# A graph layer and attention, in Winograd products: p1 written by ScalarE into the second group's PSUM bank, another order around v, q and k and of the first loads, and a last projection in plain products

**Chip, cores, metric.** One Trainium2 chip, the kernel on 1 core. The metric is device time in microseconds, the median of several executions.

## The reference, cut

```python
# x (32, 512, 512) f32, adj (512, 512) int32 of 0 and 1, about 1 in 32 set; all weights 512 x 512
def reference(x, adj, W, b, Wq, bq, Wk, bk, Wv, bv, Wo, bo):
    # layer 0
    mi, mj = x @ W[:, :512].T, x @ W[:, 512:].T
    a = adj.astype(x.dtype); deg = a.sum(axis=1)
    x = layernorm(x + deg[None, :, None] * (mi + b) + einsum('ij,bjo->bio', a, mj))
    # layer 1: 8 heads of 64
    q, k, v = heads(x @ Wq.T + bq), heads(x @ Wk.T + bk), heads(x @ Wv.T + bv)
    attn = softmax(where(adj == 0, -inf, q @ k^T / 8))
    return layernorm(x + (attn @ v) @ Wo.T + bo)
```

## The kernel before

Everything is written in the order in which each engine runs it; the schedule is by hand. A 512 x 512 product is done as seven products of 256-wide quarters (Winograd's form) in place of eight. `piece` issues one of the seven. Products 1 and 2 form group X, products 6, 7 and 4 group Y, products 5 and 3 group Z; a group adds up in one PSUM bank and each intermediate sum is read out. Product 1, p1, is needed in all three other quarters. Each of the banks a and b exists once.

```python
    def mm_tile(bank):
        return psum.tile([P, 512], FT, name="mm" + bank, bufs=1)
    GROUP = {1: "X", 2: "X", 6: "Y", 7: "Y", 4: "Y", 5: "Z", 3: "Z"}

    def piece(kind, b, i, bank):
        g = GROUP[i]
        first = (kind, b, g) not in OPEN
        if first:
            OPEN[kind, b, g] = mm_tile(bank)
        pm = OPEN[kind, b, g]
        # ... (the operands: a weight piece from the ring, a quarter or a combination)
                    nc.tensor.matmul(pm[:, c * Q:(c + 1) * Q], lhs, rhs, start=first, ...)
                    first = False
        if i == 1:
            p1 = OPEN[kind, b, "p1"] = work([P, 2, Q], "p1", 3)
            nc.scalar.copy(p1, pm)
        # ... l0, pj: GpSimd adds p1 to three quarters, VectorE adds pm to its quarter
        # ... v, q, k: product 2 is read out by ScalarE; in 6, 7, 4 VectorE adds pm and p1

    def phase_c(n):                     # v, q, k of batch n; m = n - 2 is the older batch
        # ...
        res = [norm[0], norm[1], z(apply, n, 1), z(add_bo, n, 0), pc("v", n, 1, "a")]
        if m >= 0:
            res += [z(stats, m, 1)]
        res += [pc("q", n, 1, "b"), pc("v", n, 2, "a"), pc("q", n, 2, "b")]
        if m >= 0:
            res += [z(apply, m, 1)]     # two normalisations on ScalarE; apply(m, 0) is in phase_b
        res += [norm[2], z(combos, ..., (1, 2), 0), pc("k", n, 1, "a"), norm[3], ..., pc("k", n, 2, "a")]
        if m >= 0:
            res += [z(store, m)]
        for i in ORDER[2:]:             # 6, 7, 4, 5, 3
            res += [pc("v", n, i, "a"), pc("q", n, i, "b")]
            # ...
```

`norm` are the transposes of the normalised batch, `apply` normalises two of a batch's four row blocks on ScalarE, `add_bo` adds the output bias on GpSimd, `combos` are the sums of quarters on GpSimd. In `kind`, l0 is layer 0's product (two weights, so each of its seven products takes 16 matmuls in place of 8) and pj the last projection. `told` are sums by which the kernel checks at its end whether its fast path was allowed. `ring` tiles hold weight pieces on their way to TensorE; `e` tiles hold the exponentials of the scores.

Of the kernel before, what the change touches and what calls it, by code (L numbers as in the profile page):

```python
# [25 lines left out]
def gnn_attention_kernel(  # L26
# [98 lines left out]
    nc.sync.dma_start(adj_i, rows(adj))  # L125
    wo = work([P, NC, D], "xh", 3)
    load_x(0)
    W = {}
    W["wj"] = load_w(big(), wjT, nc.scalar)
    W["wi"] = load_w(big(), wiT, nc.scalar)  # L130
    W["wv"] = load_w(work([P, NC, D], "v", 2), wvT, nc.sync)
    W["wq"] = load_w(work([P, NC, D], "v", 2), wqT, nc.scalar)
# [5 lines left out]
    nc.gpsimd.memset(mhalf, -0.5)  # L138
    b0_r = load_row("b0_r", b0)
# [5 lines left out]
    nc.gpsimd.tensor_scalar(bq_c, bq_c, QSCALE, 1.0, op0=OP.mult, op1=OP.mult)  # L145

    adj_f = big()
    nc.vector.tensor_copy(adj_f, adj_i)
# [13 lines left out]
    deg_c = const.tile([P, NC], FT, name="deg_c")  # L162
    nc.vector.reduce_sum(deg_c, adj_f, axis=AX.X)
# [8 lines left out]
    nc.scalar.copy(adjR, adjT)  # L172
# [19 lines left out]

    RING = 12
# [5 lines left out]
    def combine(name, eng):  # L199
        w = W[name]  # L200
        if name == "wq":
            nc.scalar.mul(w, w, QSCALE)
        a11, a12, a21, a22 = [w[:, 2 * j:2 * j + 2, Q * i:Q * i + Q] for i in range(2) for j in range(2)]
        s1, s2, s3, s4, n22 = [ring_tile() for _ in range(5)]
        eng.tensor_tensor(s1, a21, a22, op=OP.add)
        eng.tensor_tensor(s2, s1, a11, op=OP.subtract)
        eng.tensor_tensor(s4, a12, s2, op=OP.subtract)
        eng.tensor_tensor(s3, a11, a21, op=OP.subtract)
        nc.scalar.mul(n22, a22, -1.0)
        for i, t in ((1, a11), (2, a12), (6, s2), (7, s3), (4, n22), (5, s1), (3, s4)):  # L210
            WS[name, i] = dram.tile([P, 2, Q], FT, name=f"{name}_{i}")
            nc.sync.dma_start(WS[name, i], t)

# [112 lines left out]
    def piece(kind, b, i, bank):  # L326
# [4 lines left out]
        pm = OPEN[kind, b, g]  # L331
        terms = []
# [17 lines left out]
        p1 = OPEN[kind, b, "p1"]  # L350
        f, n = {1: (0, 0), 2: (0, 0), 6: (0, 1), 3: (0, 1), 4: (1, 0), 7: (1, 1), 5: (1, 1)}[i]
        if kind in ("l0", "pj"):
            y = XT[b]
            if i == 1:
                for n, f in ((1, 0), (1, 1), (0, 1)):
                    d = quarter(y, n, f)
                    nc.gpsimd.tensor_tensor(d, d, p1, op=OP.add)  # L357
            else:
                d = quarter(y, n, f)
                nc.vector.tensor_tensor(d, d, pm, op=OP.add)  # L360
        elif kind == "v":
            if i == 1:
                V[b] = work([P, NC, D], "v", 2)
            d = quarter(V[b], n, f)
            if i == 2:
                nc.scalar.copy(d, pm)
            elif i in (6, 7, 4):
                nc.vector.tensor_tensor(d, pm, p1, op=OP.add)
            elif i != 1:
                nc.vector.tensor_tensor(d, d, pm, op=OP.add)  # L370
        else:
            T, bias = (QT, bq_c) if kind == "q" else (KT, bk_c)
            if i != 1 and (b, f) not in T:
                T[b, f] = work([P, 2, N], kind, 3)
            if i in (6, 7):
                nc.vector.tensor_tensor(T[b, f][:, :, Q * n:Q * n + Q], pm, p1, op=OP.add)
            elif i != 1:
                for c in range(2):
                    d = T[b, f][:, c, Q * n:Q * n + Q]
                    bc = bias[:, 2 * f + c:2 * f + c + 1]  # L380
                    if i == 2:
                        nc.scalar.activation(d, pm[:, c, :], AF.Identity, bias=bc, scale=1.0)
                    else:
                        o = p1[:, c, :] if i == 4 else d
                        nc.vector.scalar_tensor_tensor(d, pm[:, c, :], bc, o, op0=OP.add, op1=OP.add)
# [4 lines left out]
    def scores(b, hp, kc):  # L390
# [7 lines left out]
        nc.scalar.activation(ps, ps, AF.Exp)  # L398
# [48 lines left out]

    PC, TR, GA = 1.73, 0.44, 1.9
# [11 lines left out]
    def phase_a(n):  # L460
# [4 lines left out]
        for i in range(max(len(g), len(k))):  # L465
            res += k[i:i + 1] + g[i:i + 1]
            if i == 1 and g:
# [20 lines left out]
    def phase_b(n):  # L488

        m = n - 2  # L490
        if n >= B:
            res = []
            for i, bank in ALONE:
                if i == 6:
                    res += [FLUSH, z(combos, TO, m, ot_quarter(m), (1, 2, 3, 4))]
                res.append(pc("pj", m, i, bank))
            return res + [z(stats, m, 0), z(stats, m, 1), z(apply, m, 0), z(apply, m, 1), z(store, m)]
        if m < 0:
            res = []
            for i, bank in ALONE:  # L500
                res.append(pc("l0", n, i, bank))
                if i == 4:
                    res += [z(stats, n, 0)]
            return res + [z(apply, n, 0), z(stats, n, 1)]
        res = []
        for i in ORDER:
# [10 lines left out]
            if i == 3:  # L517
                res.append(z(apply, m, 0))
        return res

    def phase_c(n):
# [4 lines left out]
        res = [norm[0], norm[1], z(apply, n, 1), z(add_bo, n, 0), pc("v", n, 1, "a")]  # L526
        if m >= 0:
            res += [z(stats, m, 1)]
        res += [pc("q", n, 1, "b"), pc("v", n, 2, "a"), pc("q", n, 2, "b")]
        if m >= 0:  # L530
            res += [z(apply, m, 1)]
        res += [norm[2], z(combos, TH, n, h, (1, 2), 0), pc("k", n, 1, "a"), norm[3], z(combos, TH, n, h, (1, 2), 1),
                z(combos, TH, n, h, (3, 4), 0), z(combos, TH, n, h, (3, 4), 1), z(add_bo, n, 1), pc("k", n, 2, "a")]
        if m >= 0:
            res += [z(store, m)]
        for i in ORDER[2:]:
            res += [pc("v", n, i, "a"), pc("q", n, i, "b")]
            if i == 4 and n + 1 < B and n > 0:
# [4 lines left out]

    PERIODS = [phase_a(0) + phase_b(0) + phase_c(0) + phase_a(1)]
    PERIODS += [phase_b(n) + phase_c(n) + phase_a(n + 1) for n in range(1, B)]
    PERIODS += [phase_b(B) if B > 1 else [], phase_b(B + 1)]
    for f in sum(PERIODS, []):
        if f[1] is piece:
            KEYS.extend((name, f[4]) for name in NAMES[f[2]])
# [3 lines left out]

    combine("wj", nc.gpsimd)
    combine("wi", nc.vector)

    edge = const.tile([P, NC, N], BF, name="edge")
    nc.vector.tensor_scalar(edge, adjT, 0.0, None, op0=OP.not_equal)
    nc.vector.tensor_tensor(adj_f, adjT, adjR.bitcast(FT), op=OP.not_equal)
    nc.vector.reduce_sum(told[:, B * HP:], adj_f.rearrange("p c i -> p (c i)"), axis=AX.X)  # L560
    nc.vector.tensor_scalar(told[:, B * HP:], told[:, B * HP:], 2.0 * SAFE, None, op0=OP.mult)
    combine("wv", nc.gpsimd)
    combine("wq", nc.vector)
    combine("wk", nc.gpsimd)

    pd = mm_tile("b")
    bv_w = work([P, DC, P], "big", 6)
    for dc in range(DC):
        nc.vector.tensor_scalar(bv_w[:, dc, :], ones, bv_c[:, dc:dc + 1], None, op0=OP.mult)
        nc.tensor.matmul(pd, bv_w[:, dc, :], W["wo"][:, dc, :], start=(dc == 0), stop=(dc == DC - 1))  # L570
    nc.vector.tensor_add(bo_r, bo_r, pd)
    combine("wo", nc.vector)
# [4 lines left out]
    STEPS = 2 * HP  # L577
    for n in range(1, B + 2):
        b = n - 1
        todo = PERIODS[n]  # L580
        total, done, at = sum(f[0] for f in todo), 0.0, 0
        extra = []
        for step in range(STEPS):
            if b < B:
                hp, half = divmod(step, 2)
                scores(b, hp, 2 * half)
                scores(b, hp, 2 * half + 1)
                if step > 0:
                    ph, phalf = divmod(step - 1, 2)
                    values(b, ph, phalf)  # L590
                    if phalf == 1:
                        sums(b, ph)
                        extra = rest(b, ph)
            if step == 0 and b > 0:
# [3 lines left out]
            late = [(presum, hp, half)] if b < B else []  # L598
            while at < len(todo) and done < total * (step + 1) / STEPS - 1e-6:
                if todo[at] is FLUSH:  # L600
                    while extra:
                        g = extra.pop(0)
                        g[0](*g[1:])
                else:
                    run(todo[at])
                done += todo[at][0]
                at += 1
                if todo[at - 1][0] > 0.0:

                    for g in late + (extra if step == 0 else extra[:1]):  # L610
                        g[0](*g[1:])
                    late, extra = [], [] if step == 0 else extra[1:]
# [3 lines left out]
        for f in todo[at:]:  # L616
            if f is not FLUSH:
                run(f)


    tot = const.tile([P, 1], FT, name="tot")
    nc.vector.reduce_sum(tot, told, axis=AX.X)
    pd = mm_tile("a")
    nc.tensor.matmul(pd[:, 0:1], ones, tot, start=True, stop=True)
    nc.vector.tensor_scalar(tot, pd[:, 0:1], SAFE, None, op0=OP.is_lt)
    again = const.tile([P, 1], I32, name="again")
    nc.vector.tensor_scalar(again, tot, -1.0, 1.0, op0=OP.mult, op1=OP.add)
    fast.close()
    flag = nc.values_load(again[0:1, 0:1], min_val=0, max_val=1)
    with tc.If(flag > 0), tc.tile_pool(name="general", bufs=1) as pools.work:  # L630
# [15 lines left out]
        nc.vector.tensor_scalar(nan_c, nan_c, 0.0, None, op0=OP.mult)  # L646

# [6 lines left out]
        with tc.For_i(0, B, 1) as b:  # L654
# [22 lines left out]
            for hp in range(HP):  # L677
                c = slice(hp * P, (hp + 1) * P)
                qt, kt = work([P, N], "q", 1), work([P, N], "k", 1)
                for t, w, bias, by in ((qt, wq, bq_c, QSCALE), (kt, wk, bk_c, 1.0)):  # L680
# [80 lines left out]
```

## Time and profile before

| | before |
|---|---|
| time | 4076.63 us median of 3 (4075.16 to 4078.4) |
| span of the profiled execution, mean clock | 4072.7 us, 0.992 |
| start to the first scores | 137.0 us |
| first scores to the last batch's first scores (31 batches) | 3823.8 us, 123.35 each |
| from there to the end | 111.9 us |

TensorE is busy for 95% of the span, so a change can win only in the 5% in which it waits. The lines are in the prediction. The three stretches of the table are read from the PE timeline, as the start of a score product (`sc<-q,k`) is easy to find.

### The profile page before, as it was taken

The page shows a single profiled execution, that of the slowest core. Times are in us where ns is not written, and L with a number is a line of the kernel's source. Part 1 is how long each engine was busy: PE and PEld are TensorE (multiplying, and loading weights), DVE is VectorE, ACT ScalarE, POOL GpSimd, SP SyncE. Part 2 cuts the span into 40 slices and gives each one's busy share as a digit, 9 for nine tenths or more (in the row PEclk, how much of TensorE's full clock was granted, in tenths as well). Part 3 has the DMA queues.
Part 4 walks back from the last instruction along what each step waited for, and adds up shares of the span by engine and source line. Part 5 has one row for each costly group of instructions (what it writes and reads, how often), then busy time and mean ns, then how long its engine had stood idle before and what let it go on. Part 6 is the DMA issues. An engine that isn't in the chain of part 4 may idle for free.

```text
span 4072.7 us, 47394 instructions
## 1 busy us (share of the span) xinstructions
PE 3878.7 (95%) x17442; PEld 2655.8 (65%) x17442; DVE 2604.5 (64%) x3514; ACT 1058.0 (26%) x1486; POOL 1889.5 (46%) x2010
## 2 busy tenths in 40 slices
PE   6999999999999999999999999999999999999996
PEld 4766666666666666666666666666666666666663
DVE  3576666666666666666666666666666666666665
ACT  2222222222222222222222222222222222222221
POOL 5444544545445445345454454453454444444533
PEclk8999999999999999999999999999999999999998
DMA  8333333233333333332333333333333333333330
GB/s 286 104 99 106 107 111 117 86 114 104 103 120 98 104 106 107 109 118 88 110 109 102 118 99 101 109 109 106 117 98 102 110 103 114 105 95 114 104 101 24
DMA packets 239099, 441.49 MB, mean 108 GB/s; under 512 B 23440, under 2 KB 26512, under 8 KB 238864
## 3 DMA queue, kind: packets, MB, share of 16 engines
q1 hardware_dynamic: 237024, 434.73, 35.4%
q8 instruction: 142, 2.33, 0.2%
q10 hardware_dynamic: 1584, 3.15, 0.2%
q14 instruction: 93, 0.76, 0.1%
q0 software_dynamic: 256, 0.53, 0.0%
HBM read 393.75 MB, written 44.56 MB: 108 GB/s over the span
## 4 chain that ended last, share of the span: by engine, by line
PE 70%; DVE 17%; POOL 6%; issue 3%; ACT 3%; SPq 0%; DMA 0%; POOLq 0%; ACTq 0%; DVEq 0%
PE mma L342 28%; PE mmb L342 15%; PE sc L394 9%; PE ov L416 9%; PE mmb L266 6%; DVE xh L279 5%; DVE rl L429 3%; DVE e L399 3%; POOL big L311 2%; PE ov L423 2%; DVE es L408 2%; POOL mv L235 2%; ACT xh L239 2%; PE sc L259 1%; DVE ov L434 1%
## 5 line engine op out<-in xcount | busy, mean ns | idle before, releaser
L342 PE MATMUL mma<-ring,big 128*128 128x256 f32 x5296 | 1231.1, 382 | 73.3 <-POOL big L311 30.2
L342 PEld LDWEIGHTS mma<-ring,big 128*128 128x128 f32 x5296 | 993.0, 190 | 274.8 <-POOL big L311 41.8
L398 ACT ACTIVATE sc<-sc 128x1024 f32<-128x1024 f32 x512 | 492.9, 1007 | 1645.9 <-PE sc L394 1451.8
L399 DVE TENSOR_TENSOR e<-sc,edge 128x1024 f32<-128x1024 f32 x512 | 602.3, 1218 | 359.3 <-ACT sc L398 359.3
L311 POOL TENSOR_TENSOR big<-big 128x256 f32<-128x256 f32 (+1 forms) x512 | 541.9, 1083 | 289.3 <-DVE big L260 196.7
L405 POOL TENSOR_TENSOR es<-e 128x1024 f32<-128x1024 f32 x128 | 301.2, 2353 | 736.5 <-PE ov L423 699.9
L416 PE MATMUL ov<-e,v 128*64 128x512 f32 x2048 | 500.2, 610 | 26.1 <-DVE told L434 26.1
L394 PE MATMUL sc<-q,k 64*128 64x512 f32 x2048 | 509.6, 616 | 0.4 <-ACT big L288 0.4
L429 DVE RECIPROCAL rl<-ov 128x128 f32<-128x128 f32 x512 | 458.9, 927 | 4.0 <-PE ov L423 0.2
L342 PE MATMUL mma<-big,ring 128*128 128x256 f32 x1792 | 430.2, 383 | 24.2 <-ACT p L349 20.5
L234 POOL TENSOR_SCALAR mv<-mv 128x1 f32<-128x1 f32 x256 | 78.9, 308 | 774.8 <-DVE mv L233 762.0
L342 PE MATMUL mmb<-big,ring 128*128 128x256 f32 x1792 | 432.6, 384 | 0.0
L342 PEld LDWEIGHTS mmb<-big,ring 128*128 128x128 f32 x1792 | 333.1, 190 | 113.9 <-DVE e L399 47.9
L342 PEld LDWEIGHTS mma<-big,ring 128*128 128x128 f32 x1792 | 332.2, 190 | 103.2 <-ACT p L349 27.8
L416 PEld LDWEIGHTS ov<-e,v 128*64 128x64 f32 x2048 | 125.6, 137 | 370.8 <-issue 302.1
L408 DVE TENSOR_TENSOR es<-es,e 128x1024 f32<-128x1024 f32 x256 | 313.4, 1224 | 4.4
L394 PEld LDWEIGHTS sc<-q,k 64*128 64x128 f32 x2048 | 176.4, 186 | 207.8 <-issue 194.8
L360 DVE TENSOR_TENSOR xh<-xh,mma 128x512 f32<-128x512 f32 x192 | 131.7, 686 | 264.5 <-PE mma L342 264.5
L357 POOL TENSOR_TENSOR xh<-xh,p 128x512 f32<-128x512 f32 x192 | 237.9, 1267 | 105.8 <-ACT p L349 105.1
L342 PE MATMUL mmb<-ring,big 128*128 128x256 f32 x1104 | 270.2, 389 | 15.5 <-POOL big L311 15.5
L342 PEld LDWEIGHTS mmb<-ring,big 128*128 128x128 f32 x1104 | 206.6, 192 | 94.9 <-POOL big L311 40.3
L239 ACT ACTIVATE xh<-xh,mv 128x512 f32<-128x512 f32 x256 | 201.8, 813 | 255.5 <-POOL mv L236 255.1
(106 smaller groups left out, 3634.6 us busy)
## 6 DMA issues: line engine op xcount, KB each, us to landing
ring<-wi SPq DMA_DIRECT2D x224, 256.0 KB, 2.6
ring<-wj SPq DMA_DIRECT2D x224, 256.0 KB, 2.7
ring<-wv SPq DMA_DIRECT2D x224, 256.0 KB, 2.6
ring<-wq SPq DMA_DIRECT2D x224, 256.0 KB, 2.6
ring<-wk SPq DMA_DIRECT2D x224, 256.0 KB, 2.7
ring<-wo SPq DMA_DIRECT2D x224, 256.0 KB, 2.6
xh<-in_x_dram SPq DMA_DIRECT2D x32, 1024.0 KB, 5.5
out_dram<-xh SPq DMA_DIRECT2D x32, 1024.0 KB, 5.2
```

What stands on the lines that cost most here:

```text
L239: nc.scalar.activation(y, y, AF.Identity, bias=mv[:, 4:5], scale=mv[:, 3:4])
L266: nc.tensor.matmul(pm, parts[w][:, jc, :], adjR[:, jc, :], start=(w == 0 and jc == 0), stop=(w == 1 and jc == NC - 1))
L311: nc.gpsimd.tensor_tensor(dst, p, q, op=OP.subtract)
L342: nc.tensor.matmul(pm[:, c * Q:(c + 1) * Q], lhs, rhs, start=first, stop=(kc == 1 and n == len(terms) - 1), skip_group_check=True)
L357: nc.gpsimd.tensor_tensor(d, d, p1, op=OP.add)
L394: nc.tensor.matmul(ps[:, s, :], KT[b, hp // 2][r, hp % 2, kc * P:(kc + 1) * P], QT[b, hp // 2][r, hp % 2, :], start=True, stop=True)
L398: nc.scalar.activation(ps, ps, AF.Exp)
L399: nc.vector.tensor_tensor(e, ps, edge[:, kc:kc + 1, :].to_broadcast([P, 2, N]), op=OP.mult)
L405: nc.gpsimd.tensor_add(ES[hp], E[0], E[1])
L408: nc.vector.tensor_add(ES[hp], ES[hp], E[kc])
L416: nc.tensor.matmul(PV[hp][s * HD:(s + 1) * HD, :], V[b][:, kc, c0:c0 + HD], E[kc][:, s, :], start=(kc == 0), stop=(kc == NC - 1))
L429: nc.vector.reciprocal(rl[:, c], pl[:, c])
```

## The change

Its intent: p1 is no longer added by GpSimd and VectorE, quarter by quarter. Before group Y's first product, ScalarE copies p1 into Y's bank and the products add to it. The bias of q and k moves into ScalarE's reads. The load of the next x is issued one product pair later, and its split on ScalarE now stands ahead of k's copy of p1. The first loads go on one queue with the adjacency first; most weight combinations move to VectorE beside batch 0; the last batch's projection is made of plain products per head pair.

```diff
     def piece(kind, b, i, bank):
         pm = OPEN[kind, b, g]
+        if first and g == "Y":
+            nc.scalar.copy(pm.rearrange("p (c i) -> p c i", c=2), OPEN[kind, b, "p1"])
+            first = False
...
-                for n, f in ((1, 0), (1, 1), (0, 1)):
-                    d = quarter(y, n, f)
-                    nc.gpsimd.tensor_tensor(d, d, p1, op=OP.add)
...
-            if i == 2:
+            if new:                                  # i in (2, 6, 7, 4)
                 nc.scalar.copy(d, pm)
-            elif i in (6, 7, 4):
-                nc.vector.tensor_tensor(d, pm, p1, op=OP.add)
...                                                  # phase_b
-            if i == 3:
-                res.append(z(apply, m, 0))
...                                                  # phase_c
+        res = [z(fold)] if n == 0 else []
+        res += [norm[0], norm[1], z(apply, n, 1), pc("v", n, 1, "a"), pc("q", n, 1, "b")]
         if m >= 0:
             res += [z(stats, m, 1)]
-        res += [pc("q", n, 1, "b"), pc("v", n, 2, "a"), pc("q", n, 2, "b")]
-        if m >= 0:
-            res += [z(apply, m, 1)]
+        res += [norm[2], norm[3], z(combos, TH, n, h, (1, 2)), pc("v", n, 2, "a"), pc("q", n, 2, "b"),
+                pc("k", n, 1, "a"), z(combos, TH, n, h, (3, 4)), z(add_bo, n, 0), z(add_bo, n, 1), pc("k", n, 2, "a")]
         if m >= 0:
-            res += [z(store, m)]
+            res += [z(apply, m, 0), z(apply, m, 1), z(store, m)]
...                                                  # combine: the first weights' sums
-        s1, s2, s3, s4, n22 = [ring_tile() for _ in range(5)]
+        s1, s2, s3, s4, n22 = [...]                  # halves of three of the four e buffers
...                                                  # last batch
+        for ic in range(2 * half, 2 * half + 2):
+            nc.tensor.matmul(ACC[ic], OT[B - 1, hp // 2][:, hp % 2, ic * P:(ic + 1) * P], W["wo"][:, hp, :],
+                             start=(hp == 0), stop=(hp == HP - 1))
```

## The prediction

> **What bounds the kernel now.** I read the page first, then one table of three stretches, then the waits of TensorE (PE) in the repeated part, then the order of time around the waits that the change touches.
>
> ```profile
> PE 3878.7 (95%) x17442; PEld 2655.8 (65%) x17442; DVE 2604.5 (64%) x3514; ACT 1058.0 (26%) x1486; POOL 1889.5 (46%) x2010
> ...
> 0.00:137.00 137.00, 96.79 (x424) 76.93 (x424) 49.27 (x68) 29.78 (x47) 65.78 (x73) 0.91 0.71 242
> 137.00:3960.00 3823.00, 3708.24 (x16746) 2541.56 (x16746) 2488.79 (x3354) 1005.21 (x1413) 1789.05 (x1896) 1.00 0.35 106
> 3960.00:4073.00 113.00, 73.63 (x274) 37.29 (x273) 66.47 (x92) 22.96 (x26) 34.66 (x42) 0.82 0.08 27
> ```
>
> PE is the bound. It idles 194 us in all: 40 before 137 us (prologue and batch 0), 115 in the repeated part, 39 after 3960 us (last batch). The repeated part is very regular: output stores start at 566.62 and 690.75 us, so one batch takes 124.1 us. Its PE waits from 500 to 3780 us:
>
> ```profile
> PE mma L342 <- ACT p L349: 39.0, 53, 0.8
> PE mma L342 <- POOL big L311: 25.4, 26, 1.0
> PE ov L416 <- DVE told L434: 14.1, 27, 0.5
> PE mma L342 <- DVE v L368: 8.4, 26, 0.3
> PE mma L342 <- ACT big L288: 6.4, 27, 0.2
> PE mmb L342 <- DVE oT L439: 4.7, 27, 0.4
> ```
>
> That is 98 us in 26.4 batches, 3.7 us each: .78 (second product of v) + .69 (second of k) + .97 (v6) + .52 + .33 + .24 + .17. I call the seven products of a projection v1, v2, v6 and so on. A steady batch around k and v6, ACT (ScalarE) and then PE:
>
> ```profile
> 2050.76 0.84 ACT L382 ACTIVATE q<-mmb,bq_c 128x256 f32<-128x256 f32 x2 [3.51 <-PE mmb L342]
> 2051.49 1.51 ACT L239 ACTIVATE xh<-xh,mv 128x512 f32<-128x512 f32 x2
> 2052.89 0.58 ACT L288 COPY big<-sc 128x512 f32<-128x512 f32 x1
> 2053.36 0.60 ACT L349 COPY p<-mma 128x512 f32<-128x512 f32 x1
> ...
> 2056.04 0.84 ACT L382 ACTIVATE k<-mma,bk_c 128x256 f32<-128x256 f32 x2 [1.60 <-PE mma L342]
> ...
> 2054.01 1.99 PE L342 MATMUL mma<-big,ring 128*128 128x256 f32 x8 [0.69 <-ACT p L349]
> 2056.98 1.97 PE L342 MATMUL mma<-ring,big 128*128 128x256 f32 x8 [0.97 <-POOL big L311]
> ```
>
> To see: k2 ends at 2056.00, ACT reads its bank out by 2056.88, and v6 starts .10 later in the same bank. So .97 is both the combinations on POOL and this read. Two normalisations (L239) take 1.51, and the next instruction starts 1.40 after the first of them, so .70 each in a row.
>
> [...] ACT runs in program order, .5 to .7 apart. [...] the first weight copies, issued behind the start's loads, took 11.8 us to land, a later ring load 2.6. [...] The clock is 0.50 at 30 to 40 us, where PE does nothing.
>
> **The change, part by part.**
>
> *Steady batch, removed.* POOL's six additions of p1 (6 x 1.27 = 7.6 us a batch, 238 in all), twelve small VectorE operations with a bias (12 x .48) and seven additions of p1 (7 x .69) on q, k, v; four additions of .69 come for q and k in place of small ones, so DVE loses 7.8 us a batch. Neither engine is the bound; this wins only where PE waited for it. By the built order DVE's reciprocals come one earlier, so the wait for told (.52) goes, and so does v5's for DVE (.33).
>
> *Steady batch, moved.* Rows 2 and 3 are now transposed between q1 and v2. Those .9 us of PE work lie where v2 waited .78 for ACT, so v2 waits about .05. k2 now follows k1 directly and waits for the copy of p1: .04 + .58 + .10 = .73 (before .69).
>
> *Steady batch, added.* Five copies of p1 into PSUM, .58 each, and twelve more activations out of PSUM for q and k and three copies for v. ACT goes from 26 to about 34%: no bound by load, but it is by order. In the built order of ACT stand, after the two reads of k2: FOUR normalisations of the batch two back, then the copy into v6's bank. PE has nothing between k2 and v6. So from k2's end: .04 + .73 (reads) + 4 x .70 + .58 + .10 = 4.25 us, where .97 was. And q6's copy stands behind ACT's read of v6, which waits for v6's end: .07 + .47 + .58 + .10 = 1.22 us, where nothing was. The other three copies are hidden: l0's has pj2 (1.73 us) beside it; the last projection's is ready 3.7 us after the scores start and PE needs it at 3.8; k6's has scores, values and q3 before it.
>
> Sum: .24 + .05 + .73 + 4.25 + 1.22 + .1 = 6.6 against 3.7, less about .1 for each of two fewer restarts of PE (1.99 against 1.89 after a wait): +2.6 us. Thirty batches (n = 2 to 31) have normalisations of an older batch: 30 x 2.6 = +78. The batch before them (no such normalisations) +.5.
>
> *Prologue.* The adjacency goes first on one queue; by the throughput of the first slices I take it to land at about 7 instead of 10.7 us. But the combined weights now sit in four e buffers: wi's third combination waits until a stored piece of wj has landed, behind 9.9 MB of loads (29.6 us at the trace's 385 GB/s), and ACT, in order, holds wi's last piece (about 32 us) before the copy that frees the bank of the first graph product. So:
>
> ```profile
> 62.00 3.72 PE L342 MATMUL mma<-ring,big 128*128 128x256 f32 x16 [3.60 <-DMA ring<-wi]
> ```
>
> this first weight product moves from 62 to about 42: three graph products after 33 at 2.8 each, some at half clock. Then given back: l0's p1 through SBUF into the other bank with a weight negation between them (+1.9), a wait or two in l0 for VectorE, which now carries wv, wq and wk there (+3), slow clock (+2), and the fold of bv into bo before the transposes: statistics, wo's combinations 2.8 and its operand, 6 to 7 us of waiting and 3.4 of PE. v1 starts near 81 instead of 88.7: -7. In batch 0, v6 and q6 wait +.7 and +1.2, k2 +.4: +2. Prologue: -5.
>
> *End.* Now the last batch's steps carry the projection of batch 30, the last projection is added per head pair, and no Winograd tail follows:
>
> ```profile
> 3992.78 3.32 PE L416 MATMUL ov<-e,v 128*64 128x512 f32 x8 [3.05 <-DVE told L434]
> ...
> 4045.15 3.78 PE L342 MATMUL mmb<-ring,big 128*128 128x256 f32 x8 [10.56 <-POOL big L311]
> ```
>
> I replayed it from 3960.8 with the trace's durations. Two steps of before take 16.8 us, bound by sums, four reciprocals (3.4), told (.7), values, scores. After: sums at +20.4, +38.7, +54.3 and +65.1; then six products beside the reciprocals (5.1), two more (1.7 each), four rows on DVE at 1.5 each; last row +78; POOL 1.3, ACT .8, store 2.7 and about 2 to close: +85.5. Before it took 111.9: -26.5. Plain products cost PE 16 x .86 = 13.7 instead of 28 x .43 = 12.1, but most lie in DVE's gaps.
>
> Total: 4076.6 + 78 + .5 - 5 - 26.5 = 4123.6; I say 4124.
>
> **Rivals.** (A) The p1 seeding is free and the ends win: steady part 2 us a batch better (only v2, told and v5's waits go, v6 at 1.6 or less), prologue -15, end -30: about 3970, faster. For it: ACT is 26% busy. Against it: the built order puts the four normalisations between, and ACT had idled [1.60] before k2's reads, so they can't have been done sooner only if they stand later, which they do. (B) Latency grows further: the copies for l0 and the last projection aren't hidden (their slack is about .1 us), +1 us each a batch: 30 x 2 = 60, so 4184, slower. For it: VectorE reads the bank only at 2120.3 and PE wants it at 2121.2. Against: POOL's additions[...] are gone. (C) x, loaded later by a product pair, isn't there for ACT's split, which now stands before k6's copy: I count .5 us of slack; 1 us lost would make 4155.
>
> **Range and chances.** The steady term is 78 with perhaps 20 either way, as every restart and latency counts 30 times; prologue and end +-12 each. Together about +-28: 4088 to 4156. The 2% limits are 3995 and 4158. Slower is B or C, or two of them in part: .12. Faster needs A: .03. Within: .85.
>
> **What would show it.** Right: in the waits of PE in the repeated part, v6's for ACT at 4 to 4.4 us and q6's at 1.1 to 1.3, once a batch; stores 126.7 us apart; no wait of 1 us at l0's sixth product or pj6; POOL busy some 1640 us, ACT 1350 to 1400. First weight product near 42 us, v1 near 81; from the last batch's first scores to the end 80 to 90 us. Wrong: v6 waiting under 2 us (then A), or new waits for ACT's copies elsewhere (B), or the ACT splits waiting for the load of x (C).

Marked cuts in it, and in the expectations below, are statements on the hardware that were not read from a trace or run of this case. No term of the sum is among them: 4076.6 + 78 + .5 - 5 - 26.5 = 4123.6, given as 4124. That the products add to a p1 which ScalarE has copied into their bank was an assumption when this was written; the runs were to show it.

## The result

The changed kernel took 4238.32 us (median of 4, 4235.83 to 4245.53) against 4076.74 (4 runs): ratio 1.0399, 95% interval 1.0381 to 1.0417. It is correct. A ratio here is the mean time of one kernel's fast runs over that of the other's of the same rounds, so it isn't quite the ratio of the medians quoted.

| us | before | predicted | after |
|---|---|---|---|
| start to first scores | 137.0 | -5 (with batch 0) | 140.5 (+3.5) |
| 31 batches | 3823.8 | +78.5 | 4006.5 (+182.7) |
| last first scores to end | 111.9 | -26.5 | 90.6 (-21.3) |
| profiled span | 4072.7 | +47 | 4237.5 (+164.8) |

The loss is in the repeated part: 129.24 us a batch in place of 123.35. First the busy times of the changed kernel (page, part 1), then its three stretches (us, then busy time of PE, PEld, DVE, ACT, POOL, granted clock, DMA share, GB/s):

```profile
PE 3960.3 (93%) x17418; PEld 2705.1 (64%) x17418; DVE 2395.8 (57%) x3044; ACT 1358.7 (32%) x2122; POOL 1622.0 (38%) x1677
```

```profile
0.00:140.50 140.50, 101.59 (x426) 78.73 (x426) 51.02 (x66) 35.06 (x64) 53.01 (x57) 0.91 0.63 213
140.50:4147.00 4006.50, 3791.25 (x16751) 2597.84 (x16750) 2279.41 (x2889) 1300.75 (x2032) 1546.63 (x1589) 0.97 0.34 101
4147.00:4237.00 90.00, 67.48 (x247) 28.52 (x246) 65.36 (x89) 22.88 (x26) 22.35 (x32) 0.93 0.07 24
```

Two columns matter in the middle line. PE's idle time there rose from 115 to 215 us; and PE's busy time rose as well, by 83 us against before's 3708.24, for practically the same matmuls, at a clock of 0.97 in place of 1.00. The second is what the prediction has no term for. The waits of PE from 500 to 3780 us (some 25 batches), changed kernel:

```profile
PE mma L360 <- POOL xh L307: 106.7, 25, 4.3
PE mmb L360 <- ACT mmb L348: 30.5, 25, 1.2
PE mma L360 <- ACT p L367: 16.9, 25, 0.7
PE mma L360 <- ACT big L302: 6.0, 25, 0.2
PE mmb L360 <- DVE oT L446: 4.2, 26, 0.2
PE mma L360 <- ACT mma L348: 2.7, 5, 1.2
```

All but the last are the predicted waits, to within .05 us: v6 4.27 us (predicted 4.25), q6 1.22 (1.22), k2 .68 (.73), v1 .24 and .17 for oT. The last is k6's, which the prediction called hidden (more under Rivals, below). The waits for told and of v5 are gone. The label of the first names the wrong engine, as the timeline of one batch of the changed kernel shows (start, length, engine, operation, in brackets the idle time before it and its releaser):

```profile
2014.61 1.99 PE L360 MATMUL mma<-big,ring 128*128 128x256 f32 x8 [0.68 <-ACT p L367]
2015.13 4.95 POOL L307 TENSOR_TENSOR xh<-xh,bo_r 128x512 f32<-128x512 f32 x4
2016.64 0.84 ACT L389 ACTIVATE k<-mma,bk_c 128x256 f32<-128x256 f32 x2 [2.08 <-PE mma L360]
2017.37 2.92 ACT L253 ACTIVATE xh<-xh,mv 128x512 f32<-128x512 f32 x4
2020.19 0.58 ACT L348 COPY mma<-p 128x512 f32<-128x512 f32 x1
...
2020.87 3.75 PE L360 MATMUL mma<-ring,big 128*128 128x256 f32 x8 [4.27 <-POOL xh L307]
...
2024.72 0.59 ACT L379 COPY v<-mma 128x512 f32<-128x512 f32 x1 [3.94 <-PE mma L360]
2025.20 0.59 ACT L348 COPY mmb<-p 128x512 f32<-128x512 f32 x1
2025.85 3.54 PE L360 MATMUL mmb<-big,ring 128*128 128x256 f32 x8 [1.22 <-ACT mmb L348]
...
2029.22 1.89 PE L360 MATMUL mma<-ring,big 128*128 128x256 f32 x8
```

GpSimd's bias additions (L307) end at 2020.08, ScalarE's copy of p1 into the bank (L348) at 2020.77, and v6 starts .10 after the copy: it is the copy behind four normalisations (L253) that v6 waits for. Then look at the lengths: v6 takes 3.75 us and q6 3.54, where such a product takes 1.89 to 1.99. The same batch in windows; the last figures of a line are granted clock, DMA share and GB/s:

```profile
2016.40:2020.80 4.40, 0.21 (x1) 0.00 (x0) 0.00 (x0) 4.13 (x7) 3.69 (x4) 0.77 0.18 60
2020.80:2024.60 3.80, 3.73 (x8) 2.52 (x8) 0.00 (x0) 0.00 (x0) 0.00 (x0) 0.50 0.74 276
2024.60:2025.80 1.20, 0.03 (x1) 0.00 (x0) 0.00 (x0) 1.08 (x2) 0.00 (x0) 0.50 0.12 36
2025.80:2029.40 3.60, 3.55 (x9) 2.88 (x10) 0.00 (x0) 0.00 (x0) 0.00 (x0) 0.56 0.16 61
2029.40:2035.00 5.60, 5.60 (x25) 2.50 (x25) 1.74 (x2) 3.35 (x5) 0.00 (x0) 1.00 0.35 94
```

After the idle time the clock is 0.50, through v6, q6's wait and q6. My theory after the result: **the waits cost what was predicted, and the clock that falls in the 4.27 us wait costs as much again.** Rivals: (1) the slow products come from the new form itself (accumulating onto a bank that ScalarE wrote, or DMA traffic beside v6: 276 GB/s), with no need of an idle TensorE; (2) the wait is for GpSimd's bias additions, as labelled.

### The profile page after: what moved, and what is told of

It reads as the page before. It is cut to its first block, busy times and chain, and to the rows that moved or that the text cites. A ratio compares the mean times of both kernels' runs of the same rounds, so it can differ in the third digit from the quotient of the medians.

```text
span 4237.5 us, 47155 instructions
## 1 busy us (share of the span) xinstructions
PE 3960.3 (93%) x17418; PEld 2705.1 (64%) x17418; DVE 2395.8 (57%) x3044; ACT 1358.7 (32%) x2122; POOL 1622.0 (38%) x1677
## 4 chain that ended last, share of the span: by engine, by line
PE 76%; DVE 11%; POOL 7%; DMA 2%; issue 2%; ACT 2%; SPq 0%; ACTq 0%; DVEq 0%; POOLq 0%
PE mma L360 30%; PE mmb L360 17%; PE sc L401 10%; PE ov L423 9%; PE mmb L280 5%; DVE xh L293 5%; POOL xh L307 3%; DVE rl L436 3%; POOL big L325 2%; PE ov L430 2%; DVE e L406 2%; POOL es L412 2%; DMA xh<-in_x_dram 1%; PE sc L273 1%; PE sc L301 1%
## 5 line engine op out<-in xcount | busy, mean ns | idle before, releaser
L360 PE MATMUL mma<-ring,big 128*128 128x256 f32 x5288 | 1265.7, 390 | 137.2 <-POOL xh L307 123.7
L360 PEld LDWEIGHTS mma<-ring,big 128*128 128x128 f32 x5288 | 1019.1, 195 | 327.2 <-POOL xh L307 134.5
L325 POOL TENSOR_TENSOR big<-big 128x512 f32<-128x512 f32 x384 | 525.7, 1390 | 233.9 <-DVE big L274 190.2
L360 PE MATMUL mmb<-big,ring 128*128 128x256 f32 x1792 | 480.8, 415 | 39.1 <-ACT mmb L348 39.1
L360 PEld LDWEIGHTS mmb<-big,ring 128*128 128x128 f32 x1792 | 359.5, 207 | 183.9 <-ACT mmb L348 61.0
L436 DVE RECIPROCAL rl<-ov 128x128 f32<-128x128 f32 x512 | 446.4, 917 | 5.8 <-PE ov L430 1.8
L415 DVE TENSOR_TENSOR es<-es,e 128x1024 f32<-128x1024 f32 x256 | 325.1, 1270 | 4.4
L253 ACT ACTIVATE xh<-xh,mv 128x512 f32<-128x512 f32 x256 | 198.4, 812 | 217.2 <-POOL mv L250 201.6
L183 POOL TENSOR_TENSOR xlo<-xh,xhi 128x512 fp32r<-128x512 f32 x128 | 162.6, 1281 | 237.9 <-ACT xhi L182 234.8
```

The lines of the kernel that those rows point to most:

```text
L253: nc.scalar.activation(y, y, AF.Identity, bias=mv[:, 4:5], scale=mv[:, 3:4])
L325: nc.gpsimd.tensor_tensor(dst, p, q, op=OP.subtract)
L415: nc.vector.tensor_add(ES[hp], ES[hp], E[kc])
L436: nc.vector.reciprocal(rl[:, c], pl[:, c])
```

## The experiments

Runs of one series share the runs of the kernel before (medians 4077.16, 4076.78 and 4075.82 in the three series, 7 runs each). "Changed" means the changed kernel.

**e1: the changed kernel, normalisations where before had them.**

```diff
+            if i == 3:                      # end of phase_b
+                res.append(z(apply, m, 0))
...
+        res += [..., pc("v", n, 2, "a")]
+        if m >= 0:
+            res += [z(apply, m, 1)]         # between v2 and q2
...
         if m >= 0:
-            res += [z(apply, m, 0), z(apply, m, 1), z(store, m)]
+            res += [z(store, m)]
```

> The changed kernel with the four normalisations of the older batch taken out from between the second product of k (k2) and the first seeded product of v (v6): two stand at the end of the residual stage and two between v2 and q2, as before the change. Theory 1 (ScalarE's order makes v6 wait 4.27 us, and that idle time halves TensorE's clock for the next two products): v6 waits .04 + .73 + .58 + .10 = about 1.45 us, q6 still 1.22, the clock in the repeated part goes from 0.97 back to about 1.00, batches come 2.8 + 3.6 = 6.4 us closer, so 4238 - 190 = about 4047 us. Rival 1 (the wait only, the clock falls for another reason): 4238 - 30 x 2.8 = about 4154 us and v6 and q6 still take 3.5 to 3.8 us each. Rival 2 (v6 waits for the bias addition on GpSimd, which the profile names): v6's wait stays above 4 us, 4238 us.

Measured: 4076.31 us (4073.67 to 4078.83), ratio 0.9998 (0.9981 to 1.0014). The 162 us are gone; a batch takes 123.98 us. The waits of PE, e1:

```profile
PE mma L360 <- issue: 41.5, 26, 1.6
PE mmb L360 <- ACT mmb L348: 32.0, 26, 1.5
```

v6 waits 1.60 us, and GpSimd's bias additions stand where they stood: rival 2 falls. 162 us over 30 batches are 5.4 a batch, 2.67 of it wait (4.27 - 1.60). The remaining 2.7 is clock: all of v6 take 1.96 to 1.97 and all of q6 1.99. I had expected 4047, some 30 us less, because I took 3.6 us of clock loss from the one batch shown above; the mean is 2.7.

**e3: two of the four normalisations left in the gap.**

```diff
-            res += [z(apply, m, 0), z(apply, m, 1), z(store, m)]
+            res += [z(apply, m, 1), z(store, m)]      # apply(m, 0) at the end of phase_b
```

> The changed kernel with two of the four normalisations left between k2 and v6. v6's wait 4.27 - 1.40 = 2.87 us. [...] If the loss by the clock is in proportion to the wait, it is 3.6 x 2.87 / 4.27 = 2.4 us a batch, and the run about 4160 us.

Measured: 4162.2 us (4156.13 to 4165.08), ratio 1.0212 (1.0195 to 1.0229). Against e1 that is 86 us: 30 x (2.86 - 1.60) = 38 of wait, the other 48 clock. v6 is slow in 15 of 26 batches and at full speed in the rest: with 2.86 us of idle time the loss comes in part of the batches. The total is near the 4160 of the proportion, but not by it: a batch loses the clock or it doesn't.

**e4: the changed kernel, with something for TensorE to do in the gap.** ScalarE's order stays as changed. Five products that nobody reads stand ahead of the normalisations, in a bank of the scores.

```diff
+    def filler(n):
+        pt = turn_tile()
+        for i in range(5):
+            nc.tensor.matmul(pt, ident, HT[n][:, i % DC, :], start=True, stop=True)
...
-            res += [z(apply, m, 0), z(apply, m, 1), z(store, m)]
+            res += [z(filler, n), z(apply, m, 0), z(apply, m, 1), z(store, m)]
```

> The changed kernel as it is, with five idle matmuls of 512 columns (.86 us each, 4.3 in all, result never read) given to TensorE between k2 and v6, so that it works while it waits; ScalarE's order is unchanged. Theory 1: v6 starts as late as before (within .3 us), but at full clock: v6 1.9 and q6 1.9 us in place of 3.75 and 3.54, 3.6 us a batch less, about 4130 us, mean clock near 0.99. If the slow clock does not come from the idle time: no change, 4238 us, or slower.

Measured: 4154.09 us (4151.47 to 4156.01), ratio 1.0188 (1.0171 to 1.0205): 84 us less than changed, 2.8 a batch, with useless work added (I had expected 4130, again from the 3.6 us of one batch). The timeline of PE in one batch, from k2 to q6, e4:

```profile
2106.29 1.99 PE L360 MATMUL mma<-big,ring 128*128 128x256 f32 x8 [0.68 <-ACT p L367]
2108.12 4.45 PE L550 MATMUL sc<-big,ident 128*128 128x512 f32 x10
2112.55 1.97 PE L360 MATMUL mma<-ring,big 128*128 128x256 f32 x8
2115.73 1.99 PE L360 MATMUL mmb<-big,ring 128*128 128x256 f32 x8 [1.22 <-ACT mmb L348]
```

v6 starts as late as in the changed kernel (6.26 us after k2's start in both: 2112.55 - 2106.29 and 2020.87 - 2014.61), but at full speed, with the bank written by ScalarE as in the changed kernel. So it is the idle TensorE that costs the clock. Rival 1 falls.

**e5: the kernel before, with four normalisations between ScalarE's two reads of k2.** No p1 copy into PSUM at all.

```diff
                     if i == 2:
+                        if kind == "k" and c == 1 and b > 1:
+                            apply(b - 2, 0)
+                            apply(b - 2, 1)
                         nc.scalar.activation(d, pm[:, c, :], AF.Identity, bias=bc, scale=1.0)
...                                                  # their old places
-            if i == 3:
-                res.append(z(apply, m, 0))
...
-        if m >= 0:
-            res += [z(apply, m, 1)]
```

> The kernel BEFORE, with only one thing changed: the four normalisations of the older batch stand between ScalarE's two reads of k2's bank, so that v6, which opens that bank again, waits .04 + .37 + 2.8 + .47 + .10 = about 3.8 us in place of .97. No p1 copies into PSUM. Theory 1: the same two losses appear in the old kernel, 2.8 us of wait and[...] about 3 us by the clock: 4077 + 30 x 5.8 = about 4250 us. If the slow clock belongs to the seeded banks (products that add to what ScalarE wrote): only the wait, about 4160 us.

Measured: 4205.09 us (4204.13 to 4205.55), ratio 1.0315 (1.0297 to 1.0332). v6 waits 3.79 in place of .97: 30 x 2.82 = 85 of the 128 us; the other 43 is clock, about half of what I had expected (the total came between my 4250 and the rival's 4160). The kernel before shows the same loss without the new form, another witness against rival 1.

**e9: one normalisation left in the gap** (run later, to find where the loss begins).

```diff
-            res += [z(apply, m, 1)]                    # e1, between v2 and q2
+            res += [z(apply_one, m, 2)]
...
-            res += [z(store, m)]
+            res += [z(apply_one, m, 3), z(store, m)]
```

> The changed kernel with only one of the four normalisations left between the second product of k and v6. Waits of v6 so far, with the share of batches whose v6 then ran slow (over 2.6 us): 1.60 us, 0 of 27; 2.86 us, 15 of 26; 3.79 us, 26 of 26 longer than the usual 1.97; 4.27 us, 25 of 25. One normalisation more than the 1.60 makes 2.25 to 2.35 us here. Theory: [...] the chance of the loss grows in proportion with the wait beyond some length between 1.6 and 2.86; a straight line from 15 of 26 at 2.86 to 26 of 26 at 3.79 and no lower than 1.6 gives 20 to 40% of the batches slow, a loss of 0.5 to 1.2 us a batch, and a total of 4110 to 4135 us. Rival: the loss has a limit above 2.3 us (then no batch is slow, and the total is 4096 to 4100 us from the wait alone).

Measured: 4134.36 us (4132.46 to 4138.51), ratio 1.0147 (1.013 to 1.0164). That is 58 us over e1: 30 x .56 = 17 of wait and 41 of clock. v6 waits 2.16 and is slow in 17 of 26 batches, more than I expected. The straight line was wrong, and so was the rival's limit above 2.3. I gathered from the traces (500 to 3780 us) every such product with a wait of 1 us or more ahead of it (the stretch read in one piece, so some counts differ by one from those in the expectation):

| run | wait of v6, us | slow (over 2.1 us) | mean length of v6 | slow q6 after it |
|---|---|---|---|---|
| e1 | 1.60 | 0 of 26 | 1.96 | 0 of 26 |
| e10 (below; k6) | 1.68 | 0 of 26 | 1.99 | - |
| e9 | 2.16 | 17 of 26 | 2.72 | 9 of 26 |
| e3 | 2.86 | 15 of 26 | 2.89 | 4 of 26 |
| e5 | 3.79 | 25 of 25 | 3.17 | 15 of 25 (no wait of 1 us before them) |
| changed | 4.27 | 25 of 25 | 3.26 | 22 of 25 |

In this kernel the loss begins between 1.68 and 2.16 us of idle time, and at 3.79 every batch has it. Why some batches lose and others don't, the kept traces settle, as they record when the granted clock changes. In each run all its falls from 500 to 3780 us lie on a grid of 3.413 us (in e9 they are 37, 74 or 147 steps apart). Here are two pairs of neighbouring stretches of this grid, e9:

```profile
1468.34:1471.75 3.41, 1.34 (x6) 1.24 (x7) 0.00 (x0) 1.97 (x4) 3.39 (x3) 1.00 0.51 186
1471.75:1475.17 3.41, 2.19 (x6) 1.24 (x6) 0.00 (x0) 1.08 (x2) 0.00 (x0) 0.50 0.74 274
3362.74:3366.15 3.41, 1.46 (x7) 0.95 (x5) 0.00 (x0) 1.92 (x4) 3.41 (x4) 1.00 0.44 131
3366.15:3369.57 3.41, 1.98 (x9) 1.46 (x9) 0.00 (x0) 1.19 (x3) 1.51 (x2) 1.00 0.89 332
```

(PE's busy time comes first, the granted clock third from the end.) Each pair holds a wait of v6 of 2.16 or 2.17 us. In the first TensorE is idle for 2.07 us of one stretch (3.41 - 1.34), and the next stretch has half the clock; in the second the grid cuts the wait, its first stretch has 1.95 us of idle time, and the clock stays. Over all eleven traces, from 500 to 3780 us, the clock fell after each of the 132 stretches at full clock with 2.02 us or more of idle time, and after none of the 10,184 with 1.99 us or less. From these counts I estimate that a wait of twice 2.02 us, like the changed kernel's 4.27 (25 of 25 slow), costs the clock wherever the grid cuts it, and a shorter one, like e9's 2.16 (17 of 26), only where 2.02 us or more fall into one stretch. The half clock also lasts longer in the changed kernel (two or three stretches in 22 of 25 batches) than in e5 (one in 19 of 25), which has no wait ahead of q6.

**The start: e6 and e7.** In the changed kernel the first weight product starts at 44.67 us as predicted (42), but the first scores come 3.5 us later than before. The PE timeline of its start, and then ScalarE's:

```profile
35.47 2.07 PE L280 MATMUL mmb<-adjR,xhi 128*128 128x512 f32 x4 [12.94 <-ACT big L286]
...
44.67 3.62 PE L360 MATMUL mma<-ring,big 128*128 128x256 f32 x16
...
82.87 5.63 PE L553 MATMUL mmb<-xh,big 128*128 128x512 f32 x8 [5.94 <-DVE big L552]
```

```profile
34.31 0.63 ACT L219 ACTIVATE e<-big 128x512 f32<-128x512 f32 x1 [14.33 <-DMA wj<-e]
34.85 0.57 ACT L286 COPY big<-mmb 128x512 f32<-128x512 f32 x1
```

ScalarE holds one weight's last sum until a piece of the other weight has been stored from an e buffer, and the copy that frees the graph product's bank stands behind it. e6 puts those sums into ring tiles again; e7 also makes the operand of the fold of bv early and puts its matmuls after batch 0's projections.

```diff
-        s1, s2, s3, s4, n22 = [...]        # e buffers
+        s1, s2, s3, s4, n22 = [ring_tile() for _ in range(5)] if name in ("wi", "wj") else [...]
```

> The changed kernel with one thing undone: the combinations of the first two weights are written into ring tiles again, as in the kernel before, so that none of them waits until a stored piece has left an e buffer. My theory of the start: the 12.94 us wait of the second graph product for ScalarE is this wait for a buffer. Then that wait is gone or under 4 us, the first weight product starts at 36 to 40 us instead of 44.67, and 4 to 8 us of it stay in the total: 4230 to 4234 us. Rival: what holds the product is the landing of the weights themselves; then it stays within 2 us of 44.67 and the total at 4238 us. The repeated part stays as it is in both: waits of 4.27 and 1.22 us for v6 and q6.

Measured: 4231.57 us (4230.62 to 4235.05). The first weight product starts at 38.38, the first scores at 134.21 (changed 140.48): 6.3 us, as expected. The wait of the second graph product shrank from 12.94 to 6.90 us only, not to the 4 or less of my theory; the trace puts the rest down to GpSimd's sums of the other weight, which no run takes away.

```diff
-        res = [z(fold)] if n == 0 else []
...
+            if i == 7 and n == 0:
+                res += [z(fold_ready)]               # VectorE: wo's sums and the operand
+        if n == 0:
+            res += [z(fold), z(add_bo, n, 0), z(add_bo, n, 1)]   # the matmuls, later
```

> The one before, and also the fold of bv into bo split: wo's combinations and the operand are made by VectorE beside batch 0's projections, and the four matmuls of the fold and both additions of bo stand at their end instead of ahead of batch 0's transposes. My theory: the fold cost TensorE a wait of 5.94 us and 5.63 us of matmuls ahead of v1 at 89.67 us; then v1 starts at 70 to 79 us, batch 0's first scores at 122 to 132 us instead of 140.48, and the total is 4219 to 4230 us. Rival: batch 0 is bound there by VectorE, which has the same work either way; then v1 is early, but the first scores come at 138 us or later and the total stays above 4232 us.

Measured: 4232.23 us (4230.28 to 4234.56), no gain over e6. v1 starts at 72.67 in place of 83.39, and the first scores at 134.16, the same. By the trace, the 10.7 us are given back where GpSimd's additions of bo now stand ahead of batch 1's split. The PE timeline, e7:

```profile
106.82 3.70 PE L560 MATMUL mmb<-xh,big 128*128 128x512 f32 x8 [0.78 <-DVE q L393]
...
117.56 1.53 PE L281 MATMUL mmb<-adjR,xlo 128*128 128x512 f32 x4 [3.94 <-POOL xlo L183]
118.88 3.26 PE L361 MATMUL mma<-big,ring 128*128 128x256 f32 x8
```

The fold's 3.5 us, a wait of 3.94 for GpSimd's split (xlo), and slow products after it (3.26 us where 1.89 to 1.99 is usual). Neither of my two theories named GpSimd.

**e8: keep the p1 copies and take TensorE's waits away.** The start of e7; the normalisations of the older batch as in e1; each copy of p1 (`seed`) is issued one product before its bank is needed, and q's products stand between those of k and v. The load of the next x is issued earlier too, which no run tests alone (under Rivals, below, is what it can be worth).

```diff
+        res += [norm[2], norm[3], z(combos, TH, n, h, (1, 2, 3, 4)), pc("v", n, 2, "a")]
+        if m >= 0:
+            res += [z(apply, m, 1), z(store, m)]
+        res += [pc("q", n, 2, "b"), z(seed, "q", n, "b"), pc("k", n, 1, "a"), pc("q", n, 6, "b"), pc("k", n, 2, "a"),
+                z(seed, "v", n, "a"), pc("q", n, 7, "b"), pc("v", n, 6, "a")]
+        ... load of the next x, additions of bo, batch 0's fold_ready
+        res += [pc("v", n, 7, "a"), pc("q", n, 4, "b"), pc("v", n, 4, "a"), pc("q", n, 5, "b"), pc("v", n, 5, "a")]
+        ... the next batch's split
+        res += [pc("q", n, 3, "b")]
+        ... batch 0's fold
+        return res + [pc("v", n, 3, "a")]
...                                           # phase_a: the seed of k first, then gather, k6, gather, k7 ...
+        res = [z(seed, "k", n - 1, "a")] if n > 0 else []
-            res += k[i:i + 1] + g[i:i + 1]
+            res += g[i:i + 1] + k[i:i + 1]
```

> The start of the one before, and a steady order that keeps the p1 copies into PSUM but never lets TensorE wait for them: the older batch's normalisations stand where the kernel before had them, each copy of p1 is issued one product before its bank is needed, and products of q lie between those of k and v. My theory (the loss is the waits for ScalarE's queue, and the clock that the 4 us wait costs): no wait of 1 us or more is left on the products of v, q, k; about 1.2 to 1.6 us of waits a batch in all; the mean granted clock from 500 to 3780 us is 0.99 to 1.00; a batch takes 121 to 122 us instead of 129.2; total 3965 to 3995 us, faster than the kernel before by 2 to 3%. Rival: seeding the bank costs TensorE something by itself (the accumulating matmuls are slower[...]): then a batch stays at 123 us or above and the total at 4030 us or above.

Measured: **3944.84 us** (3944.26 to 3946.43), correct, ratio 0.9679 to the kernel before (0.9662 to 0.9695). A batch takes 120.10 us, against 123.35 before and 129.24 changed. All waits of PE from 500 to 3780 us, e8:

```profile
PE mma L364 <- DVE k L396: 21.1, 27, 0.8
PE mma L364 <- ACT big L303: 6.4, 27, 0.2
```

About 1.0 us a batch is left, against 3.7 before and 6.6 changed, and no product is slow. It came out below my 3965 to 3995. Of the 3.9 us a batch less than e1 (123.98), 3.0 are waits (4.07 against 1.04); the rest is busy time of TensorE (219.8 ns a matmul from 500 to 3780 us against 221.4, at a clock of 1.00 in both), for which I have only an argument, fewer restarts. Seeding the bank costs TensorE nothing that the trace shows: the products that add to it take 1.89 to 1.99. The assumption behind the copies holds too: all nine kernels here that copy p1 into the bank are correct. In the chain that ended last (page, part 4) PE now has nearly all, e8:

```profile
PE 96%; DVE 2%; ACT 1%; POOL 1%; issue 0%; DMA 0%; SPq 0%; ACTq 0%; DVEq 0%; POOLq 0%
```

**e10: e8 with the copies late again**, each just ahead of its product.

```diff
-        res = [z(seed, "k", n - 1, "a")] if n > 0 else []
-        ..., z(seed, "q", n, "b"), ...  and  z(seed, "v", n, "a"), ...
```

> The fast version of the last series with one thing taken back: each copy of p1 into PSUM stands again just ahead of the product that needs it, instead of one product earlier. If the early copies are what keeps TensorE busy there, q6 waits for the copy of k1's result and its own copy (0.04 + 0.58 + 0.58 + 0.10 = 1.3 us), v6 for the read of q7 and its copy (0.04 + 0.84 + 0.58 + 0.10 = 1.6 us): 2.9 us more a batch, no loss of clock (no wait above 1.6 us), 3945 + 31 x 2.9 = 4035 us, within 4020 to 4055. Rival: the new order of products and the normalisations' old place did it all: then under 3965 us.

Measured: 4094.26 us (4093.22 to 4095.78), ratio 1.0046 (1.003 to 1.0063). The early copies are worth 149 us, more than the whole lead of e8 over before. The waits, e10:

```profile
PE mma L364 <- ACT mma L343: 80.6, 52, 1.7
PE mmb L364 <- issue: 31.6, 26, 1.2
```

q6 1.22 (expected 1.3), v6 1.42 (1.6), and k6 1.68, which I had left out: its copy stands behind ScalarE's copy and cast for the gather (.58 and .62). These three are 4.3 us of the 4.7 that a batch became longer (124.81 against 120.10), and none cost the clock (no product slow in 26 waits of 1.68; mean clock of the run 0.997).

## Why the prediction was wrong

It said 4124 (4088 to 4156, slower .12); the run took 4238. By its own steps:

- **Steady batch, the sum 6.6 against 3.7: right as a sum of waits, wrong as a time.** The waits measured from 500 to 3780 us are 4.27 + 1.22 + .68 + .24 + .17 and little else, 6.6 (the sum is one of 2.7 more, not 2.6: 6.6 - 3.7 - .2). The four normalisations in one row ahead of the copy, ScalarE's running in the built order (the copy at 2020.19 after the normalisations at 2017.37 to 2020.29) and the disappearance of the waits for told and of v5 came as worked out. GpSimd's and ScalarE's load came too: 1622 us (some 1640) and 1358.7 (1350 to 1400).
- **The step that failed is the missing factor in "+2.6 us": what TensorE does after the wait.** The prediction had read a clock of 0.50 at 30 to 40 us of before, where PE does nothing, and counted slow clock in the start only (+2), although it had just derived an idle time of 4.25 us in every batch. Measured: v6 3.26 us and q6 3.45 on average, in place of 1.97 and 1.99, so 2.75 a batch. Times 30: 83 us. e4 (filled gap, -84 us) and e1 show it. With it, the prediction would have been 4124 + 83 = 4207, and slower.
- **"About .1 each for fewer restarts"** is too small for these runs to show.
- **The rest of the repeated part.** In the middle line of the stretches, idle time grew by 100 us and busy time by 83. So 83 is the clock, in line with the 83 from the products. The other 100 are some 21 above the 78.5: 10.3 of them are waits of k6 (under Rivals), about 3 the rounded sum, and the 6 of two fewer restarts a batch don't show in the busy time.
- **Start, -5: measured +3.5.** The first weight product came at 44.67 (42 predicted) and the wait for the stored piece is real (e6). Too small were l0's waits (5.4 in all, 3.02 of it for GpSimd's combinations, where I had 3 for VectorE) and the fold's matmuls, 5.63, part of it at half clock (0.50 from 82.87 to 86.8 us), where I had 3.4; its wait of 5.94 came near the 6 to 7. v1 began at 89.67, not near 81. But the 81 was also added up wrongly: 42, the 26.7 that before takes from its first weight product to v1, and the terms given back make 85 to 86, and the prologue about -1. And 9.9 MB at 385 GB/s are 25.7 us; the 29.6 can only be a time from the start, some 4 us more (in before, 11 GB/s moved from 0 to 2 us and 243 from 2 to 4).
- **End, -26.5: measured -21.3.** Sums of the last head pair came at +69.3 us (65.1 predicted), after a wait of 4.83 for VectorE's oT ahead of the plain products; from there to the end it was 21.3 (20.4, although the terms after its last row, 78, make 84.8 and not 85.5). The mechanism was right.
- **Rivals.** A lost for the reason given against it, the order; yet e8 shows that its main claim, that the p1 copies can be free, is true in another order, and its 3970 was near e8's 3945 by chance, as e8 has another order. B didn't happen: neither l0's sixth product nor the projection's waits. C happened in part, and I had overlooked it. In 30 batches ScalarE's split of the next x waits for its load, by 1.05 to 8.96 us, and in eight of them k6, whose copy stands behind the split, then waits too: 10.3 us in all. The .5 us of slack was there in most batches only. One of the eight, ScalarE's timeline and then PE's, changed kernel:

```profile
2051.11 1.14 ACT L182 CAST xhi<-xh 128x512 fp32r<-128x512 f32 x2 [2.63 <-DMA xh<-in_x_dram]
2052.16 0.58 ACT L348 COPY mma<-p 128x512 f32<-128x512 f32 x1
2052.79 1.99 PE L360 MATMUL mma<-big,ring 128*128 128x256 f32 x8 [0.78 <-ACT mma L348]
```

In e1 these waits of k6 are 12.0 us; in e8 and e10, which issue the load earlier, the split never waits for it. A rival "the new wait is long enough to cost the clock" was missing; it would have been the right one.

## What to carry to other kernels

When a change makes TensorE wait longer at once, don't price only the wait: ask what the products after it will take. Here no product was slow after 1.68 us and 17 of 26 were after 2.16, and in the changed kernel the slow ones cost 83 us beside 100 us of added waits. Here an engine that is 32% busy (ScalarE) held up the one that is 93% busy, by what stands ahead in its queue; print the built order and look at what is between the release of a buffer and its refill. Issue the copy that prepares a bank one product earlier and put another product between: here the same operations ran in 4238, 4094 and 3945 us in three orders.
